# A four-layer graph network on one core: x fetched behind older adjacency codes, DMA transposes on the planner's wire, layer 3's preparation first

## The chip, the cores and the metric

The kernel runs on one NeuronCore of a Trainium2 chip. The core has a matrix engine (TensorE, PE in the profile), a vector engine (VectorE, DVE), an engine for activation functions (ScalarE, ACT), a small general one (GpSimd, POOL), and SyncE (SP), which here only issues DMAs. Each engine works through its own list of instructions in order and waits on semaphores where its operands come from another engine. Copies between the main memory and the on-chip memory are done by 16 DMA engines. The metric is the device time in microseconds; lower is better. The time before is 2350.49 us, the median of three runs (2347.99 to 2351.76).

## What is computed

32 graphs, each with 512 nodes of 256 features (`x`) and a 512x512 adjacency of zeros and ones (`adj`), go through four attention layers. Each layer normalises, clips at zero, runs its own kind of graph attention over the adjacency, and adds the result to x. All in float32. Cut to what matters:

```python
for layer in (L0, L1, L2, L3):
    h = relu(layernorm(x));  x = x + layer(h, adj)

# L0: A = softmax(h att_W h^T / 16 + mask); twice: x = tanh(A (x W + b))
# L1: Wh = h W^T; e = leaky(src_i + dst_j); softmax over neighbours; A Wh
# L2: as L1 with exp(-leaky(...)), rows divided by their sum; elu
# L3: h = feat W
#     logits = (h a_1)^T + h a_2 + (h a_12) h^T
#     e = leaky(logits); softmax over neighbours
#     elu(feat W_1 + (attention feat) W_2)
```

For layer 3 the kernel forms `M = W a_12 W^T` once, so that the logits are `feat M feat^T`. This needs W turned, a product with a_12, and a second product: the preparation that is moved below.

## The kernel before

**One plan for everything.** The kernel doesn't emit instructions as it goes. Every piece of work of every graph is an `op`: its engine ("PE", "V", "A", "G", or "D" for a DMA issued by SP), its cost as a pair (how long it holds the engine, when its result is there), what it comes after, and which buffers it uses from small pools (34 pages of 4 KB a partition, 8 PSUM banks, 5 value buffers and a few more). `Plan.order` (L134) then plays a list scheduler over all ops: each gets a due time, and on each engine the ready op with the earliest due time goes next if its buffers are free. The resulting order is the order of the instructions in each engine's list. A plan's "after" orders the issue; on the chip only true dependences of data and buffers become semaphores.

**Due times.** The ops of graph `g` get `g * apart` as their due time; the last two graphs get another distance, `apart_last`. From there each op's due time is moved forward by the costs of what follows it. `Plan.best` (L93) tries 16 values of `apart` with 4 of `apart_last`, lets `replay` (L111) play each order with the plain costs, and takes the best.

**The wire.** An op with a `size` shares one modelled wire with all others that have one: it ends when the wire has carried its bytes, at 200 bytes per ns, plus 2000 ns. Loads of x, adj and the row spreads have a size. A DMA transpose has none: it costs `D_TURN = (1310.0, 2600.0)` whatever else is on the wire.

**A graph's work.** SP fetches x (512 KB) and adj (four tiles of 256 KB). VectorE makes codes of adj (L522), DMA transposes turn them (`codeT`, L525). In each layer VectorE takes statistics of x, GpSimd the root (`rstd`), ScalarE normalises (`xn`, L573); VectorE, or ScalarE in layer 1, splits it into two 16-bit planes (L578), a DMA transpose turns each tile (`planesT`, L581), and ScalarE joins them (`hT`, L593). Then come products of features (banks f, L877), of values (banks v, L903), of scores (q, s), and attention (banks a, L761 and L838; z and o for layer 0's second convolution). Most of these are done by a scheme of seven half-size products, in which PE's next product into a bank waits until ScalarE has written the bank's content out (`fa`, `v`, `y`, `w`). Layer 3's softmax needs a maximum over rows, made with two more DMA transposes (`crest`, L1168). For graph 0, codes and layer 0's xn are turned on TensorE instead of by DMA.

**When x is fetched.** The plan lets the x of graph b go after the x of graph b-2, as soon as a page is free and fewer than seven graphs are underway.

**Preparation of the weights.** It is a part of the plan, as work of graph 0. GpSimd loads the weights after graph 0's adjacency (`load`, L345). `transposed` (L363) turns a matrix with TensorE through a bank; `product` (L379) multiplies; VectorE copies the banks out. Layer 3's W and a_12 are two such loads; W is turned (four 128x128 transposes), and two products of 256x256 give `awt` and `m3_sb`. ScalarE loads b0, its first table, and warms it up (L432 to L434) before the plan begins.

```python
    t = transposed(l3_sb, wt3, [load(l3_sb, rows_of(l3_w), "raw2")], "raw2", "raw4")
    a = product(lambda d: awt()[:, d, :], a12_sb, lambda c: wt3()[:, c, :], H,
                t + [load(a12_sb, rows_of(l3_a12), "raw3")], "raw3", "raw4", "raw5")
    a = product(lambda d: m3_sb()[:, d, :], wt3, lambda c: awt()[:, c, :], H, a, "raw4", "raw5", "raw6")
```

Of the kernel before, what the change touches and what calls it, by code (L numbers as in the profile page):

```python
# [15 lines left out]
AF = mybir.ActivationFunctionType  # L16
# [3 lines left out]
P = 128  # L20
# [27 lines left out]
A_NORM, A_JOIN, V_SPLIT = (491.0, 590.0), (620.0, 767.0), (332.0, 422.0)  # L48
D_TURN = (1310.0, 2600.0)
V_SQUARES = (180.0, 270.0)  # L50
D_OUT, D_SPREAD = (550.0, 2500.0), (550.0, 4500.0)
# [4 lines left out]
class Plan:  # L56
# [9 lines left out]

    APART, APART_LAST = [1000.0 * k for k in range(32, 64, 2)], [1000.0 * k for k in (2, 5, 8, 12)]
    HOP = 100.0
    LAND, RATE = 2000.0, 200.0
# [23 lines left out]
    def best(self, pools):  # L93
        for o in self.ops:
            o["depth"] = 0
        again = True
        while again:
            again = False
            for o in self.ops:
                depth = max((a["depth"] + 1 for a in o["after"]), default=0)  # L100
                again |= depth > o["depth"]
                o["depth"] = max(depth, o["depth"])
        apart = min(itertools.product(self.APART, self.APART_LAST), key=lambda a: self.replay(self.order(pools, *a)))
        out = self.order(pools, *apart)
        took = self.replay(out)
        assert took < float("inf"), "the plan is stuck"
        return out, took
# [25 lines left out]

    def order(self, pools, apart, apart_last):  # L134
        free = {pool: list(range(n)) for pool, n in pools.items()}
# [8 lines left out]
        for o in self.ops:  # L144
            for p in o["uses"]:
                p["users"] += 1
        last = max(o["graph"] for o in self.ops)
        for o in self.ops:
            late = max(0, o["graph"] - last + 2)
            o["due"] = (o["graph"] - late) * apart + late * apart_last  # L150
        for o in sorted(self.ops, key=lambda o: -o["depth"]):
# [57 lines left out]
def kernel(  # L209
# [153 lines left out]

    def transposed(w_sb, dst, after, *keys):
        done = []
        for c in range(HC):
            key = f"bank{next(banks)}"

            def turn(c, key):
                for r in range(HC):  # L370
                    w = w_sb()[:, r, c * P : (c + 1) * P] if len(w_sb().shape) == 3 else w_sb()[:, r, c, :]
                    nc.tensor.transpose(W[key][:, r * P : (r + 1) * P], w, ident)

            def out_of(c, key):
                p = W[key][:, : HC * P]
                nc.vector.tensor_copy(dst()[:, c], p if len(dst().shape) == 3 else p.rearrange("p (i k) -> p i k", i=2))

            a = prepare("PE", pe(nt=HC), after, partial(turn, c, key), key, *keys)
            done.append(prepare("V", V_ADD, [a], partial(out_of, c, key), key, *keys))  # L379
        return done  # L380

    def product(dst, wT, rhs, cols, after, *keys):

        done = []
        for d in range(HC):
            key = f"bank{next(banks)}"

            def multiply(d, key):
                for c in range(HC):
                    nc.tensor.matmul(W[key][:, :cols], wT()[:, c, d * P : (d + 1) * P], rhs(c),  # L390
                                     start=(c == 0), stop=(c == HC - 1))

            def out_of(d, key):
                nc.vector.tensor_copy(dst(d), W[key][:, :cols])

            cost = pe(n256=2 * HC) if cols > P else pe(nt=2 * HC)
            a = prepare("PE", cost, after, partial(multiply, d, key), key, *keys)
            done.append(prepare("V", V_ADD, [a], partial(out_of, d, key), key, *keys))
        return done
# [28 lines left out]
    for n, dst, w, key in (("w0", w0_s, w0, "raw9"), ("att", att_s, att_w, "raw10")):  # L428
# [4 lines left out]
    warm = const.tile([P, 1], F32, tag="warm", name="warm")  # L433
    nc.scalar.activation(warm, zero, AF.Exp)  # L434
    ready["w1"] = [load(w1_sb, rows_of(w1))]
# [11 lines left out]
         for i in range(2)]  # L447
# [5 lines left out]

    t = transposed(l3_sb, wt3, [load(l3_sb, rows_of(l3_w), "raw2")], "raw2", "raw4")
    a = product(lambda d: awt()[:, d, :], a12_sb, lambda c: wt3()[:, c, :], H,
                t + [load(a12_sb, rows_of(l3_a12), "raw3")], "raw3", "raw4", "raw5")
    a = product(lambda d: m3_sb()[:, d, :], wt3, lambda c: awt()[:, c, :], H, a, "raw4", "raw5", "raw6")
    ready["m3"] = seven_of(m3_sb, m3, HALF, a, "raw6")
# [18 lines left out]

    def graph(b, adj_before, x_before):

# [23 lines left out]
        def fetch_adj(t):  # L503
            nc.sync.dma_start(out=T["adj"][:, t, :], in_=adj[b, t * P : (t + 1) * P, :])


        got_x = [op("D", D_X, [x_before], partial(fetch_x, ts), "x", "ahead", size=P * H * 4 * (ts.stop - ts.start))
                 for ts in ([slice(t, t + 1) for t in range(NT)] if b == 0 else [slice(0, NT)])]
# [27 lines left out]
        for g in range(NT // 2):  # L536
            code = op("V", V_CODE, [got_adj[2 * g + 2], code], partial(classes, g), "adj", "code", "slot")
            for t in (2 * g, 2 * g + 1):
                if b:
                    coded.append(op("D", D_TURN, [code], partial(turn_code, t), "code", "codeT"))  # L540
                else:
                    key = f"bank_c{t}"
                    a = op("PE", pe(nt=NT), [code], partial(turn_code_pe, t, key), "code", key)
                    coded.append(op("V", V_MASK, [a], partial(code_of, t, key), key, "codeT"))
# [10 lines left out]
        def normed(l, xs):  # L555
# [41 lines left out]
            for g in range(NT // 2):  # L597
# [7 lines left out]
                for t in (2 * g, 2 * g + 1):  # L605
                    flat, over = f"planes{l}_{t}", f"planesT{l}_{t}"
                    a = op("A", A_NORM, [r], partial(norm, t), "x", f"xn{l}")
                    if b == l == 0:

                        key = f"bank_n{t}"  # L610
                        a = op("PE", pe(nt=2 * HC), [a], partial(turn_pe, t, key), f"xn{l}", key)
                        done.append(op("V", V_ADD, [a], partial(out_of, t, key), f"hT{l}", key))
                        continue
                    a = op("A" if l in BYACT else "V", A_JOIN if l in BYACT else V_SPLIT, [a], partial(split, t), f"xn{l}", flat)
                    a = op("D", D_TURN, [a], partial(turn, t), flat, over)
                    done.append(op("A", A_JOIN, [a], partial(join, t), over, f"hT{l}"))
# [574 lines left out]
        a = op("V", (334.0, 425.0), hi, highest, "crest3")  # L1191
        a = op("D", D_TURN, [a], partial(turn, 0, 2), "crest3")
        a = op("V", (900.0, 1000.0), [a], tops, "crest3")
        a = op("D", D_TURN, [a], partial(turn, 1, 0), "crest3")
        row = op("A", A_PRELU2, [a], leaky_row, "crest3")
# [69 lines left out]

    code, got_x = None, [None, None]
    for b in range(B):
        code, got = graph(b, code, got_x[-2])
        got_x.append(got)
# [37 lines left out]
```

## Time and profile before

| | us |
|---|---|
| median of three runs | 2350.49 |
| lowest, highest | 2347.99, 2351.76 |
| the profiled execution, its own time | 2347.43 |
| its span, first to last instruction | 2345.7 |
| VectorE busy | 2111.6 |
| ScalarE busy | 1704.1 |
| first matmul starts | 8.58 |
| last matmul ends | 2339.78 |

The span is what the trace shows; 1.7 us of the execution lie outside of it. Sums from the trace stand against 2347.43, and that execution is 3.1 us below the median. The granted clock of TensorE is 0.998 on average. Idle time of an engine that isn't the bound costs nothing by itself: GpSimd waits 1,615.7 us in all for `ve`, and nothing is late for it.

The second part of the page gives the DMA engines' share of busy time in 40 slices of 59 us. It is highest at the start, where all weights and the first graphs' inputs come in:

```profile
DMA  7431233323333233333333343233342333321221
GB/s 192 96 77 35 57 78 81 83 60 84 86 75 88 62 79 82 74 85 83 75 71 85 74 88 79 61 87 79 79 90 63 78 82 72 89 50 39 52 49 43
```

### The profile page before, as it was taken

To read this page: it belongs to the slowest core of one execution; us is meant where nothing else is said; L and a number is where in the kernel's file an instruction comes from. 1 tells how busy PE (TensorE), PEld (TensorE's weight loads), DVE (VectorE), ACT (ScalarE), POOL (GpSimd) and SP (SyncE) were. 2 spreads that over 40 slices of the span, in tenths; PEclk is the share of its full clock that TensorE was granted. 3 is DMA by queue.
4 is the path that set the end of the run, shared out by engine and by line. 5 is a ranking of instruction groups with operands and counts; after the bars stand their busy time and mean duration, and the time that the engine had idled before them with its cause. 6 is when DMAs were issued, how large, how long until landed. Compare 5 with 4: busy or idle time off the path is not lost.

```text
span 2345.7 us, 38186 instructions
## 1 busy us (share of the span) xinstructions
PE 2314.3 (99%) x13022; PEld 1999.0 (85%) x13022; DVE 2111.6 (90%) x5316; ACT 1704.1 (73%) x3273; POOL 268.6 (11%) x343
## 2 busy tenths in 40 slices
PE   7999999999999999999999999999999999999998
PEld 5888888888888898888888888988888888888887
DVE  6878899999999999999999899998999999987898
ACT  5667787667787667877777876677866778676884
POOL 3000101110110110111101111101111011010110
PEclk9999999999999999999999999999999999999999
DMA  7431233323333233333333343233342333321221
GB/s 192 96 77 35 57 78 81 83 60 84 86 75 88 62 79 82 74 85 83 75 71 85 74 88 79 61 87 79 79 90 63 78 82 72 89 50 39 52 49 43
DMA packets 429860, 178.31 MB, mean 76 GB/s; under 512 B 384128, under 2 KB 401664, under 8 KB 429664
## 3 DMA queue, kind: packets, MB, share of 16 engines
q1 hardware_dynamic: 424288, 157.51, 31.2%
q0 software_dynamic: 5232, 18.23, 2.3%
q8 instruction: 103, 1.69, 0.3%
q14 instruction: 93, 0.76, 0.1%
q10 hardware_dynamic: 144, 0.13, 0.0%
HBM read 67.64 MB, written 16.89 MB: 36 GB/s over the span
## 4 chain that ended last, share of the span: by engine, by line
PE 89%; ACT 6%; DVE 3%; DMA 2%; issue 1%; SPq 0%; ACTq 0%; DVEq 0%
PE bank_a L761 27%; PE bank_z L1012 7%; PE bank_s3p L1136 5%; PE bank_q0p L968 5%; PE bank_v0p L903 4%; PE bank_f0p L877 4%; PE bank_f3p L877 4%; PE bank_o L1030 4%; PE bank_w3p L903 4%; PE bank_a3p L838 4%; PE bank_q0q L968 3%; PE bank_s3q L1136 3%; PE bank_a3q L838 3%; PE bank_v1p L903 2%; PE bank_v3p L903 2%; PE bank_v2p L903 2%
## 5 line engine op out<-in xcount | busy, mean ns | idle before, releaser
L761 PE MATMUL bank_a<-v,e 128*128 128x258 f32 (+2 forms) x3232 | 819.3, 382 | 1.8 <-ACT e L1188 0.7
L761 PEld LDWEIGHTS bank_a<-v,e 128*128 128x128 f32 x3232 | 578.5, 191 | 78.8 <-issue 11.6
L573 ACT ACTIVATE xn<-x,off,rstd 128x256 f32<-128x256 f32 x512 | 279.4, 600 | 215.2 <-DVE off L569 214.8
L593 ACT COPY hT<-planesT 128x512 uint16<-128x512 uint16 x508 | 386.6, 773 | 48.7 <-DMA planesT<-planes 47.8
L566 POOL TENSOR_TENSOR rstd<-ve,mhalf 128x2 f32<-128x2 f32 x256 | 230.5, 912 | 1643.5 <-DVE ve L563 1615.7
L1012 PE MATMUL bank_z<-e,y 128*128 128x512 f32 x512 | 239.9, 593 | 0.9 <-ACT y L1003 0.9
L560 DVE BATCH_NORM_STATS2 st<-x 128x6 f32<-128x512 f32 x256 | 177.2, 697 | 5.8 <-DMA x<-in_x_dram 4.8
L578 DVE COPY planes<-xn 128x512 uint16<-128x512 uint16 x380 | 155.6, 421 | 25.5 <-DMA planesT<-planes 16.1
L735 ACT ACTIVATE e<-row,v 128x512 f32<-128x512 f32 x224 | 159.0, 734 | 0.2 <-DMA row<-row 0.2
L1012 PEld LDWEIGHTS bank_z<-e,y 128*128 128x128 f32 x512 | 89.7, 191 | 66.6 <-issue 57.4
L738 ACT ACTIVATE e<-e 128x1024 f32<-128x1024 f32 x128 | 137.5, 1075 | 0.1
L1030 PE MATMUL bank_o<-w_sb,zT 128*128 128x256 f32 x512 | 120.4, 379 | 0.0
L1143 DVE SCALAR_TENSOR_TENSOR e<-bank_s3p,v,mask 128x256 f32<-128x256 f32 x256 | 111.4, 477 | 8.9 <-PE bank_s3p L1136 7.8
L976 ACT ACTIVATE e<-e 128x512 f32<-128x512 f32 x124 | 78.1, 635 | 50.8 <-DVE e L987 49.6
L667 DVE TENSOR_TENSOR hs<-hT,hs 128x256 f32<-128x256 f32 x254 | 106.1, 418 | 0.5
L1030 PEld LDWEIGHTS bank_o<-w_sb,zT 128*128 128x128 f32 x512 | 95.4, 190 | 12.0
L698 ACT COPY v<-bank_v2p 128x258 f32<-128x258 f32 x128 | 47.4, 370 | 76.3 <-PE bank_v2p L903 76.0
L670 DVE TENSOR_TENSOR hs<-hT 128x512 f32<-128x512 f32 x127 | 86.9, 685 | 10.7 <-ACT hT L593 10.6
L1185 DVE TENSOR_TENSOR e<-e,crest 128x1024 f32<-128x1024 f32 x64 | 77.0, 1218 | 20.0 <-ACT crest L1179 20.0
L979 DVE TENSOR_TENSOR e<-bank_q0p,mask 128x512 f32<-128x512 f32 x124 | 84.8, 684 | 8.7 <-PE bank_q0p L968 8.5
L1231 ACT ACTIVATE r<-y,one 128x512 f32<-128x512 f32 (+1 forms) x65 | 46.5, 715 | 56.2 <-DVE y L1241 47.9
L1050 DVE SCALAR_TENSOR_TENSOR e<-codeT,e 128x1024 f32<-128x1024 bf16 x64 | 78.0, 1220 | 9.8 <-ACT e L738 9.3
(225 smaller groups left out, 5400.4 us busy)
## 6 DMA issues: line engine op xcount, KB each, us to landing
adj<-in_adj_dram SPq DMA_DIRECT2D x128, 256.0 KB
x<-in_x_dram SPq DMA_DIRECT2D x31, 512.0 KB
out_dram<-y POOLq DMA_DIRECT2D x31, 512.0 KB, 3.4
row<-row SPq DMA_DIRECT2D x56, 256.0 KB
planesT<-planes SPq DMA_TRANSPOSE x508
codeT<-code SPq DMA_TRANSPOSE x124
crest<-crest SPq DMA_TRANSPOSE x64
row<-sT SPq DMA_DIRECT2D x56, 2.0 KB
```

The costliest lines, as they stand in the source:

```text
L560: nc.vector.bn_stats(T[f"st{l}"][:, g, :], T["x"][:, two(g), :].rearrange("p t h -> p h t"))
L566: nc.gpsimd.tensor_tensor(T[f"rstd{l}"][:, two(g)], T[f"ve{l}"][:, two(g)], mhalf[:, two(g)], ALU.pow)
L573: nc.scalar.activation(T[f"xn{l}"][:, t, :], T["x"][:, t, :], AF.Relu, bias=T[f"off{l}"][:, t : t + 1], scale=T[f"rstd{l}"][:, t : t + 1])
L593: nc.scalar.copy(bits[:, :, :, t * P : (t + 1) * P], T[f"planesT{l}_{t}"].rearrange("p (b c) n -> p b c n", b=2))
L761: nc.tensor.matmul(T[key][:, : LEAD + H + 1 - lead], e(l, c)[:, t * P : (t + 1) * P], T[f"v{l}"][:, c, lead:], start=(c == 0), stop=(c == ...
L838: nc.tensor.matmul(p[:, i * WIDE : i * WIDE + k], a[:, j, i * P : (i + 1) * P], b_[:, j, :], start=fresh and i == j == 0, stop=True, skip_ ...
L877: nc.tensor.matmul(p[:, : N // 2], w[:, x - 1, :], right(x), start=fresh, stop=True, skip_group_check=True)
L903: nc.tensor.matmul(p[:, j * k : (j + 1) * k], right(x)[:, j * P : (j + 1) * P], w[:, x - 1, :], start=fresh and j == 0, stop=True, skip_gr ...
L968: nc.tensor.matmul(p[:, j * N // 2 : (j + 1) * N // 2], right(x)[:, j * P : (j + 1) * P], left(x), start=fresh and j == 0, stop=True, skip ...
L1012: nc.tensor.matmul(T[f"bank_z{k}"], T["y0"][:, c, k * P : (k + 1) * P], e(0, c), start=(c == 0), stop=(c == NT - 1))
L1030: nc.tensor.matmul(T[key][:, j * H : (j + 1) * H], T["zT"][:, k, t * P : (t + 1) * P], w1_sb[:, k, :], start=(k == 0), stop=(k == HC - 1))
L1136: nc.tensor.matmul(p[:, j * N // 2 : (j + 1) * N // 2], left(x)[:, j * P : (j + 1) * P], right(x), start=fresh and j == 0, stop=True, skip ...
```

## The change

Four things are changed. The order of all instructions is made anew by the plan, so each of them moves instructions on every engine.

1. The x of graph b now also comes after the last op of the codes of graph b-2 (`codes_before`).
2. The DMA transposes of codes, planes and crest have a `size` (128 KB each), so they share the plan's wire.
3. Layer 3's W and a_12 are loaded by ScalarE (`early`), right after b0 and before its table is loaded; the warm-up of the table comes behind them as an op of the plan. Transposing W and the two products are evacuated by ScalarE (`by="A"`) instead of VectorE.
4. `Plan.best` starts from the same grid of distances, and then moves the due times of groups of graphs: the first one to four together, and the last one to eight together, by 8, 4 and 2 us either way, keeping each move that makes `replay` shorter.

```diff
+A_ISSUE, LANDING, A_WARM = (400.0, 400.0), (0.0, 3600.0), (1480.0, 1480.0)
...
+    STEPS = [8000.0, 4000.0, 2000.0]
...
-        apart = min(itertools.product(self.APART, self.APART_LAST), key=lambda a: self.replay(self.order(pools, *a)))
-        out = self.order(pools, *apart)
-        took = self.replay(out)
+        graphs = max(o["graph"] for o in self.ops) + 1
+
+        def took_by(starts):
+            return self.replay(self.order(pools, starts))
+
+        def spread(apart, apart_last):
+            return [(g - max(0, g - graphs + 3)) * apart + max(0, g - graphs + 3) * apart_last for g in range(graphs)]
+
+        starts = min((spread(*a) for a in itertools.product(self.APART, self.APART_LAST)), key=took_by)
+        took = took_by(starts)
+        early = [slice(0, g + 1) for g in range(4)]
+        late = [slice(g, graphs) for g in range(graphs - 1, graphs - 9, -1)]
+        for step in self.STEPS:
+            for which, way in itertools.product(late[:5] + early + late[5:], (step, -step)):
+                moved = list(starts)
+                moved[which] = [t + way for t in moved[which]]
+                t = took_by(moved)
+                if t < took:
+                    starts, took = moved, t
+        out = self.order(pools, starts)
...
-            late = max(0, o["graph"] - last + 2)
-            o["due"] = (o["graph"] - late) * apart + late * apart_last
+            o["due"] = starts[o["graph"]]
...
+    def copied(by, dst, src):
+
+        if by == "A":
+            nc.scalar.copy(dst, src)
+        else:
+            nc.vector.tensor_copy(dst, src)
...
-            done.append(prepare("V", V_ADD, [a], partial(out_of, c, key), key, *keys))
+            done.append(prepare(by, A_HALF if by == "A" else V_ADD, [a], partial(out_of, c, key), key, *keys))
...
     warm = const.tile([P, 1], F32, tag="warm", name="warm")
-    nc.scalar.activation(warm, zero, AF.Exp)
+
+    def early(dst, src, key):
+
+        a = prepare("A", A_ISSUE, [], lambda: nc.scalar.dma_start(out=dst(), in_=src), key)
+        return a, prepare("L", LANDING, [a], lambda: None, key)
...
-    t = transposed(l3_sb, wt3, [load(l3_sb, rows_of(l3_w), "raw2")], "raw2", "raw4")
+    l3_here, a12_here = early(l3_sb, rows_of(l3_w), "raw2"), early(a12_sb, rows_of(l3_a12), "raw3")
+    prepare("A", A_WARM, [l3_here[0], a12_here[0]], lambda: nc.scalar.activation(warm, zero, AF.Exp))
+    t = transposed(l3_sb, wt3, [l3_here[1]], "raw2", "raw4", by="A")
     a = product(lambda d: awt()[:, d, :], a12_sb, lambda c: wt3()[:, c, :], H,
-                t + [load(a12_sb, rows_of(l3_a12), "raw3")], "raw3", "raw4", "raw5")
-    a = product(lambda d: m3_sb()[:, d, :], wt3, lambda c: awt()[:, c, :], H, a, "raw4", "raw5", "raw6")
+                t + [a12_here[1]], "raw3", "raw4", "raw5", by="A")
+    a = product(lambda d: m3_sb()[:, d, :], wt3, lambda c: awt()[:, c, :], H, a, "raw4", "raw5", "raw6", by="A")
...
-    def graph(b, adj_before, x_before):
+    def graph(b, adj_before, x_before, codes_before):
...
-        got_x = [op("D", D_X, [x_before], partial(fetch_x, ts), "x", "ahead", size=P * H * 4 * (ts.stop - ts.start))
+        got_x = [op("D", D_X, [x_before, codes_before], partial(fetch_x, ts), "x", "ahead", size=P * H * 4 * (ts.stop - ts.start))
...
-                    coded.append(op("D", D_TURN, [code], partial(turn_code, t), "code", "codeT"))
+                    coded.append(op("D", D_TURN, [code], partial(turn_code, t), "code", "codeT", size=P * N * 2))
...
-                    a = op("D", D_TURN, [a], partial(turn, t), flat, over)
+                    a = op("D", D_TURN, [a], partial(turn, t), flat, over, size=P * H * 4)
...
-        a = op("D", D_TURN, [a], partial(turn, 0, 2), "crest3")
+        a = op("D", D_TURN, [a], partial(turn, 0, 2), "crest3", size=P * N * 2)
...
-        a = op("D", D_TURN, [a], partial(turn, 1, 0), "crest3")
+        a = op("D", D_TURN, [a], partial(turn, 1, 0), "crest3", size=P * N * 2)
...
-    code, got_x = None, [None, None]
+    codes, got_x = [None, None], [None, None]
     for b in range(B):
-        code, got = graph(b, code, got_x[-2])
+        code, got = graph(b, codes[-1], got_x[-2], codes[-2])
+        codes.append(code)
```

More of the change, by code (lines that the diff above doesn't have):

```diff
@@ L132, in replay, with order @@
         return max(end.values())
-    def order(self, pools, apart, apart_last):
+    def order(self, pools, starts):
         free = {pool: list(range(n)) for pool, n in pools.items()}
@@ L146, in order @@
                 p["users"] += 1
-        last = max(o["graph"] for o in self.ops)
         for o in self.ops:
-            late = max(0, o["graph"] - last + 2)
-            o["due"] = (o["graph"] - late) * apart + late * apart_last
+            o["due"] = starts[o["graph"]]
         for o in sorted(self.ops, key=lambda o: -o["depth"]):
@@ L362, in halves, with transposed @@
         return w.rearrange("p c (i k) -> p c i k", i=2)[:, :, :, 1:]
-    def transposed(w_sb, dst, after, *keys):
+    def copied(by, dst, src):
[3 more added lines that the diff above has]
+            nc.vector.tensor_copy(dst, src)
+    def transposed(w_sb, dst, after, *keys, by="V"):
         done = []
@@ L375, in out_of, with product @@
                 p = W[key][:, : HC * P]
-                nc.vector.tensor_copy(dst()[:, c], p if len(dst().shape) == 3 else p.rearrange("p (i k) -> p i k", i=2))
+                copied(by, dst()[:, c], p if len(dst().shape) == 3 else p.rearrange("p (i k) -> p i k", i=2))
             a = prepare("PE", pe(nt=HC), after, partial(turn, c, key), key, *keys)
-            done.append(prepare("V", V_ADD, [a], partial(out_of, c, key), key, *keys))
+            done.append(prepare(by, A_HALF if by == "A" else V_ADD, [a], partial(out_of, c, key), key, *keys))
         return done
-    def product(dst, wT, rhs, cols, after, *keys):
+    def product(dst, wT, rhs, cols, after, *keys, by="V"):
         done = []
@@ L393, in out_of @@
             def out_of(d, key):
-                nc.vector.tensor_copy(dst(d), W[key][:, :cols])
+                copied(by, dst(d), W[key][:, :cols])
             cost = pe(n256=2 * HC) if cols > P else pe(nt=2 * HC)
             a = prepare("PE", cost, after, partial(multiply, d, key), key, *keys)
-            done.append(prepare("V", V_ADD, [a], partial(out_of, d, key), key, *keys))
+            done.append(prepare(by, A_HALF if by == "A" else V_ADD, [a], partial(out_of, d, key), key, *keys))
         return done
```

## The prediction

> **What bounds the kernel now.** I read the engine totals first, then the chain of waits, then TensorE's own waits, then the stages, and last the timeline where a wait stood out.
>
> ```profile
> PE 2314.3 (99%) x13022; PEld 1999.0 (85%) x13022; DVE 2111.6 (90%) x5316; ACT 1704.1 (73%) x3273; POOL 268.6 (11%) x343
> PE 89%; ACT 6%; DVE 3%; DMA 2%; issue 1%; SPq 0%; ACTq 0%; DVEq 0%
> ```
>
> TensorE is the bound: 99% busy and 89% of the chain. But "busy" hides small holes, because ends of matmuls are modelled. I want the work it must do, so I take start-to-start times from a saturated stretch of the timeline:
>
> ```profile
> 1202.07 1.03 PE L1136 MATMUL bank_s3p<-hs,fs 128*128 128x256 f32 x4
> 1202.93 1.03 PE L761 MATMUL bank_a<-v,e 128*128 128x258 f32 x4
> 1203.80 0.61 PE L903 MATMUL bank_w3p<-l_w1s,hT 128*128 128x128 f32 x4
> 1204.24 1.04 PE L761 MATMUL bank_a<-v,e 128*128 128x258 f32 x4
> ```
>
> Four passes of 256 columns take 0.86 us, four of 258 take 0.87, four of 128 take 0.44: 216, 217.5 and about 112 ns a pass; 512 columns take 429 (four in 1.72 us in the chain). Times the counts by shape (3,190 of 256, 3,232 of 257 to 259, 536 of 512, some 6,030 of 128 to 130, a few small ones) this is 2,300.2 us. Both compiled kernels hold the same passes, so neither gets below it. The span of 2,345.7 is then: 8.6 before the first matmul, 5.9 after the last, and 30.8 of holes. Summing start-to-start time minus cadence by stage, the holes are 4.4 us up to 28.5, 4.9 from there to 50, 0.6 to 100, 11.0 from 100 to 2150 and 10.0 after that. Everything this change can win is in those 45 us; its own first-order effect on TensorE's work is nil. The stages and the waits agree:
>
> ```profile
> 0.00:8.58 8.58, 0.00 (x1) 0.01 (x1) 2.28 (x8) 2.14 (x4) 2.38 (x17) 1.00 0.70 218
> 8.58:28.50 19.92, 19.38 (x64) 10.95 (x65) 15.58 (x50) 8.97 (x16) 12.03 (x16) 1.00 0.87 235
> 28.50:50.00 21.50, 18.80 (x74) 13.88 (x75) 15.01 (x47) 15.11 (x31) 6.71 (x9) 0.92 0.79 172
> ```
> ```profile
> PE bank_n L586 <- ACT xn L573: 9.0, 2, 8.6
> PE bank_f3p L877 <- ACT fa L887: 5.2, 7, 1.2
> PE bank_f0p L877 <- ACT fa L885: 2.0, 1, 2.0
> PE bank_a3p L838 <- DVE e L814: 1.3, 1, 1.3
> ```
>
> Columns of a stage: its time, then busy time of PE, PEld, DVE, ACT, POOL, then clock, DMA share, GB/s. The DMA engines are 70 to 87% busy in the first 50 us. The start's chain names what they hold up, and the timeline shows what is behind the second wait, for one graph in the middle:
>
> ```profile
> 20.17 7.08 DMA planesT<-planes
> 27.28 0.77 ACT hT L593
> 28.08 6.04 DMA planesT<-planes
> ```
> ```profile
> 1327.40 0.77 ACT L593 COPY hT<-planesT 128x512 uint16<-128x512 uint16 x1 [1.22 <-DMA planesT<-planes]
> 1329.18 0.48 ACT L887 ACTIVATE fa<-bank_f3p,l_u 128x256 f32<-128x256 f32 x1
> 1329.71 0.70 PE L877 MATMUL bank_f3p<-hT,m 128*128 128x256 f32 x2 [0.88 <-ACT fa L887]
> ```
>
> Two DMA transposes took 7.1 and 6.0 us at the start. Later ScalarE, which works in order, stood 1.22 us before a late transpose, evacuated the f3 bank late, and TensorE stood 0.88 us. That stall comes back every fourth graph (at 758, 1044, 1330 and 1616 us: 0.57, 0.90, 1.04, 1.35, together 3.9).
>
> **What the Trainium skill says.** "DMA: Bandwidth & Descriptors", section "Queues, rings and completion order": each DMA engine serves the rings of SP and ScalarE in turn, by packets. So loads on ScalarE's ring take bandwidth from x on SP's; the trace of before has only 0.13 MB on ScalarE's ring and can't show it. Its section "Issuing engines are not separate DMA queues" says that a second issuer saves only issue time. "TensorE: Matmul & The Clock Gate", section "What's actually happening": the array starts at half clock until about 3.4 us of busy time. The trace agrees: graph 0's first eight 256-column passes take 3.65 us (456 ns each against 216).
>
> **The change part by part.**
>
> *Layer 3's W and A first.* Removed from GpSimd: two issues at 26.4 and 27.2 us (0.74 and 0.77 us); GpSimd is 11% busy, so that is nothing. Added on ScalarE: two issues at the 0.41 us of its b0 issue, so table load (1.28) and warm (0.20) end near 3.5 us instead of 2.7; ScalarE is idle until 7.92 anyway: nothing. Moved: 4 transposes and 16 passes, 4 x 0.112 + 16 x 0.216 = 3.9 us of TensorE, from a full stretch to the front, where it has 8.6 us of idleness; and six 128x256 copies, 0.42 each on VectorE, to ScalarE at about 0.38, 2.3 us. In the compiled order ScalarE makes four of these copies before graph 0's first xn, so graph 0 waits for W, the transposes, A and the first product. The cost: W issued near 1.2 to 1.6 lands near 5.5 to 6.5 us (x's first tiles, issued from 0.74, were used at 5.46, and 512 KB more now share the engines: at 235 to 380 GB/s 1.4 to 2.2 us for whatever comes behind, x of graph 1 among it). Transposes and copies to about 7.8, eight passes at the cold 0.456 to 11.4, so xn starts near 11.5 where it was 7.92, and the first n at 12.2 where it was 8.58. That is 3.6 lost. Against it: 3.9 of work is done, the cold stretch is paid by it and not by graph 0 (8 x 0.24 = 1.9), and the 0.4 waits between the n pairs are filled by the second product (some 0.5). Net gain 2.7; I take 3. Ends: W at 4.5 us gives 5; A late by 3 us gives 0; VectorE waiting for x of graph 1 before the second offset, behind all loads, gives -2.
>
> *x behind the codes two graphs back.* This is in the plan alone. In the compiled SP queue it moves x of graphs 2 and 3 from before graph 0's adjacency to behind graph 1's first transposes and behind adj 1, and x 4 to 6 behind adj 3 to 5. From graph 8 on each x stands at the same place as before (x 19 still between layer 1's and layer 2's transposes), so there it is nothing. At the start four x of 0.5 MB leave the first 24 us, some 7 us of the engines at 300 GB/s. The transposes of 7.1 and 6.0 us should fall towards the 3.3 to 4.4 us that the same wait has later in the chain. The holes from 28.5 to 50 are 4.9; ScalarE's wait for those transposes ended 2.2 of it, the reduced clock after it about 1.5. I take 2.5 of it as won. Against: graphs 2 to 5 filled TensorE while graph 0 went through its chain alone, and they now come later. I placed both orders on the cadence scale: graph 3's first f0 moves from 43 to 84 us, graph 4's from 134 back to 112; graph 0 has v1 at 63 (was 59), but f3 at 165 (was 176). Distances in graph 0's chain (o0 to v1: 21 us against 19; a1 to v2 17 against 20; v2 to a2 9 against 15) leave the 4 to 5 us of leaky, exp and mask covered. So -0.5. Sum of this part 2; ends -4 (fillers missing) and 4.
>
> *Transposes on the plan's wire, and due times moved graph by graph.* No instruction is added; the order changes all the way. In the table of stages the order of before repeats every four graphs, the new one every graph (f3 of graphs 12, 13, 14, 15 at 1013, 1084, 1156, 1227 us). At the f3 of graph 16, ScalarE now writes two fa blocks before it turns to hT of graph 20 (before: one, then hT, exp, the second), and SP issues both of graph 20's first transposes ahead of the row spread, not one. That is the stall above, so I count 3.9 as mostly gone, and half of the other 7.1 between 100 and 2150: 3.5 + 3.5 less 2 for new ones = 5. Ends: 9 and, by the rival below, -14. In the tail the last 22 us of matmuls are the same in both orders, one by one, and stages from graph 29's a2 on stand within 1 us; the 5.9 after the last matmul stay. Of the 10 us of holes I take 1; ends -3 and 4.
>
> Sum: 3 + 2 + 5 + 1 = 11 on the profiled execution's 2347.4 (span 2345.7 and 1.7 around it): 2336.4. The median of the runs shown is 3.1 above that execution, so 2339.5 by the median; I say 2339. What is late next is TensorE itself, still with some 20 us of holes.
>
> **Rivals.** (A) Only the start gains, the rest stays as it is: 5 us, 2345.5. For it: the tail hardly moves, the middle was planned already. Against: the order that stalled is rearranged at exactly that place. (B) Slower: one stall in every graph. Graph 12's stages in the new order stand within 1 us of those of before's graph 12, and that is one of the stalling ones; the others are now copies of it. If f3 or another bank then waits 0.9 us in each of some 20 graphs, that is 18 us in place of 3.9, against 6 won elsewhere: 2350.5 + 14 - 6 = 2358.5. It decides from 20 x s - 3.9 - 6 > 4.7, so s above 0.73 us a graph. For it: VectorE is 46 to 48 us busy in 50 there, little slack. Against: the two changes of queue order named above, and before's 50 us windows with no hole at all. (C) Prep in front costs graph 0 more than it frees (W or A at 8 us or later): start -4, middle +5, rest 1: 2348.5. (D) It doesn't do what it says: the x rule is inert after the start; that is in the forecast already.
>
> **How the numbers follow.** Forecast, 2334 to 2344: 0.56. A: 0.17. B: 0.15. C: 0.12. Low end: all good ends together (5 + 4 + 9 + 4 = 22) would give 2328.5; I take 2330. High end: 2353 leaves B's upper part out. A measurement of this kernel can tell 0.2%, 4.7 us, from no change: 2345.8 and 2355.2 are the borders. Faster: forecast 0.56, most of A 0.11, a little of C 0.04: 0.71. Same: rest of A, most of C, B's lower edge: 0.15. Slower: 0.14.
>
> **What would show it.** Right: first matmul near 6 us, sixteen passes with about 450 ns at the front, first xn at 11 to 12, attention of graph 0 (a0) near 27 to 28 though 3.9 us more work precede it; planesT pairs of 3 to 4 us there; f3's 5.2 us of waits under 2.5; DMA share of the second slice lower. Wrong: a PE wait repeated every 71.4 us; PE idle between 40 and 130 us; W's landing after 8 us.

## The result and the profile after

| | before | after |
|---|---|---|
| median of the runs (four each) | 2351.12 | 2325.88 |
| lowest, highest | 2347.99, 2355.23 | 2325.32, 2327.81 |
| ratio of the times, 95% interval | | 0.9892 [0.9878, 0.9907] |
| the profiled execution, its own time | 2347.43 | 2327.81 |
| TensorE's holes, by the sum used in the prediction | 30.8 | 12.7 |

The kernel became 25 us faster; 11 were forecast, and 2325.88 lies below the range of 2330 to 2353. In the profiled executions the difference is 19.6 us. The other 5.6 come from where these two executions stand among their runs: before's is 3.7 below the median of its four runs here (3.1 below that of the three known then), after's is the slowest of its four, 1.9 above theirs.

The first, second and fourth parts of the page of after (engine totals, slices, shares of the chain):

```profile
PE 2307.2 (99%) x13022; PEld 1996.3 (86%) x13022; DVE 2113.0 (91%) x5310; ACT 1720.1 (74%) x3279; POOL 257.5 (11%) x341
...
DMA  6441233423333323333233333233332333321221
...
PE 92%; ACT 3%; DVE 2%; DMA 1%; issue 0%; SPq 0%; ACTq 0%; DVEq 0%
```

The same 13,022 passes run. The chain has 3% more of TensorE, 3% less of ScalarE. The second DMA digit stays at 4. The stages of the start (columns as before: its time, busy time of PE, PEld, DVE, ACT, POOL, clock, DMA share, GB/s):

```profile
0.00:8.58 8.58, 1.31 (x5) 0.94 (x6) 0.76 (x2) 2.08 (x4) 1.00 (x15) 1.00 0.68 214
8.58:28.50 19.92, 19.89 (x75) 12.40 (x76) 16.67 (x52) 10.42 (x21) 10.38 (x13) 1.00 0.81 208
28.50:50.00 21.50, 21.50 (x95) 15.88 (x94) 13.08 (x45) 11.11 (x22) 3.88 (x5) 1.00 0.46 108
```

From 28.5 to 50 TensorE is full (18.8 of 21.5 before), and the DMA engines are 46% busy there instead of 79%. TensorE's waits of after (what it waited for: total, times, longest):

```profile
PE bank_w L396 <- DMA raw_w<-in_L_gnn_W_dram: 7.2, 1, 7.2
PE bank_f3p L907 <- ACT fa L917: 0.9, 2, 0.7
```

The stall at f3 has gone from 5.2 us in seven waits to 0.9 in two. Where it came from, the longest pieces of the two chains tell. Before had these, one every four graphs, and the next at 1608.91 (start, length, what):

```profile
752.19 3.34 DMA planesT<-planes
...
1037.05 4.35 DMA planesT<-planes
...
1322.89 4.49 DMA planesT<-planes
```

Among the 40 longest pieces of after's chain no `planesT` is left; its only DMAs are layer 3's W at the start and a few others:

```profile
1.17 5.93 DMA raw_w<-in_L_gnn_W_dram
...
1021.95 4.74 DMA codeT<-code
```

One line misleads. This is ScalarE's wait for the transposes in before, and then in after:

```profile
ACT hT L593 <- DMA planesT<-planes: 47.8, 58, 3.4
```
```profile
ACT hT L623 <- DMA planesT<-planes: 47.0, 52, 6.5
```

The sum is the same. I therefore took every join (ScalarE's `hT`) that had waited for its transpose, and measured from the start of SP's issue to the start of the join. Before, 36 of 61 took over 3 us (median 3.41, longest 7.78); after, 11 of 53 (median 2.49, longest 5.08). The quick ones are joined after 2.42 to 2.55 us. In before, 24 of the 36 late ones had a DMA other than a transpose issued in the 4 us ahead of them, and 2 of the 18 quick ones; in after, 2 of the 11 late ones, so loads aren't the whole of it. ScalarE still waits for 47 us. That it now does so mostly where TensorE needs nothing from it is inferred from TensorE's own waits; it wasn't followed wait by wait.

By stage, with the prediction's sum of holes (start-to-start time less cadence; a few hundredths below zero are rounding of the cadence), one profiled execution each:

| us | before first matmul | to 28.5 | to 50 | to 100 | 100-2150 | after 2150 | after last matmul |
|---|---|---|---|---|---|---|---|
| before | 8.6 | 4.4 | 4.9 | 0.6 | 11.0 | 10.0 | 5.9 |
| after | 7.2 | 3.2 | 0.0 | 0.6 | 3.5 | 5.3 | 5.8 |
| won | 1.3 | 1.2 | 4.9 | -0.1 | 7.5 | 4.7 | 0.1 |

The prediction's sum counts slow passes as holes too. Twice in before, right after stalls, the granted clock (third column from the right) was about one half for 3.4 us:

```profile
36.20:39.60 3.40, 3.40 (x12) 2.85 (x11) 2.24 (x11) 3.13 (x8) 3.28 (x5) 0.50 0.58 79
2200.20:2203.70 3.50, 3.50 (x13) 3.06 (x13) 3.50 (x6) 2.41 (x5) 0.35 (x1) 0.51 0.17 33
```

Most passes of 257 and 258 columns start every 427 to 431 ns there instead of every 217, which makes about 1.7 us of the 4.9 and 1.7 of the 10.0. The execution of after has no such stretch before its last matmul.

### The profile page after: what moved, and what is told of

It is laid out like the page before. It is cut to its first block, busy times and chain, and to the rows that moved or that the text cites. A ratio compares the mean times of both kernels' runs of the same rounds, so it can differ in the third digit from the quotient of the medians.

```text
span 2326.0 us, 38151 instructions
## 1 busy us (share of the span) xinstructions
PE 2307.2 (99%) x13022; PEld 1996.3 (86%) x13022; DVE 2113.0 (91%) x5310; ACT 1720.1 (74%) x3279; POOL 257.5 (11%) x341
## 4 chain that ended last, share of the span: by engine, by line
PE 92%; ACT 3%; DVE 2%; DMA 1%; issue 0%; SPq 0%; ACTq 0%; DVEq 0%
PE bank_a L791 28%; PE bank_z L1042 8%; PE bank_s3p L1166 5%; PE bank_q0p L998 5%; PE bank_o L1060 4%; PE bank_v0p L933 4%; PE bank_f0p L907 4%; PE bank_w3p L933 4%; PE bank_f3p L907 4%; PE bank_a3p L868 4%; PE bank_s3q L1166 3%; PE bank_q0q L998 3%; PE bank_a3q L868 3%; PE bank_v1p L933 2%; PE bank_v2p L933 2%; PE bank_v3p L933 2%
## 5 line engine op out<-in xcount | busy, mean ns | idle before, releaser
L596 POOL TENSOR_TENSOR rstd<-ve,mhalf 128x2 f32<-128x2 f32 x256 | 222.4, 899 | 1737.6 <-DVE ve L593 1537.6
L623 ACT COPY hT<-planesT 128x512 uint16<-128x512 uint16 x508 | 375.9, 771 | 47.4 <-DMA planesT<-planes 47.0
L608 DVE COPY planes<-xn 128x512 uint16<-128x512 uint16 x380 | 155.4, 419 | 13.6 <-DMA planesT<-planes 8.2
L700 DVE TENSOR_TENSOR hs<-hT 128x512 f32<-128x512 f32 x127 | 86.9, 684 | 11.7 <-ACT hT L623 11.3
L1080 DVE SCALAR_TENSOR_TENSOR e<-codeT,e 128x1024 f32<-128x1024 bf16 x64 | 78.0, 1219 | 12.5 <-ACT e L768 12.4
L1111 DVE SCALAR_TENSOR_TENSOR e<-codeT,e 128x1024 f32<-128x1024 bf16 x64 | 77.9, 1218 | 6.6 <-ACT e L768 6.5
```

The lines of the kernel that those rows point to most:

```text
L596: nc.gpsimd.tensor_tensor(T[f"rstd{l}"][:, two(g)], T[f"ve{l}"][:, two(g)], mhalf[:, two(g)], ALU.pow)
L623: nc.scalar.copy(bits[:, :, :, t * P : (t + 1) * P], T[f"planesT{l}_{t}"].rearrange("p (b c) n -> p b c n", b=2))
```

## The experiments

The theory after the result: the transposes' `size` brings most of it, at the start and in the tail too, since it tells the planner which transposes will be late (in the tail this is a guess: before has one late join there). The rival: each part has its own share at its own place, as the prediction had it.

**One part left out of the change.** The edits to the changed kernel, one for each run (`no_early` also puts back the two GpSimd loads, VectorE's copies and the early warm-up):

```diff
# no_gate
-        got_x = [op("D", D_X, [x_before, codes_before], partial(fetch_x, ts), "x", "ahead", size=...)
+        got_x = [op("D", D_X, [x_before], partial(fetch_x, ts), "x", "ahead", size=...)
# no_early
-    t = transposed(l3_sb, wt3, [l3_here[1]], "raw2", "raw4", by="A")
+    t = transposed(l3_sb, wt3, [load(l3_sb, rows_of(l3_w), "raw2")], "raw2", "raw4")
# no_size, at all four DMA transposes
-                    a = op("D", D_TURN, [a], partial(turn, t), flat, over, size=P * H * 4)
+                    a = op("D", D_TURN, [a], partial(turn, t), flat, over)
# no_search
-    STEPS = [8000.0, 4000.0, 2000.0]
+    STEPS = []
```

> All of the change but the rule that x comes behind the codes two graphs back. Theory P (each part has its own place): the early x are back in front of the first adjacency, transposes of 6 to 7 us come back there and the holes from 0 to 50 us go from 3.2 to about 8; the middle and the tail stay; 2331. Theory O (the gain is the order that the search of due times finds, the parts hardly matter): within 2 us of 2326.

> All of the change but layer 3's early loads and preparation. Theory P: first matmul back at 8.6 us, graph 0's first passes at 450 ns, 3.9 us of preparation back in the full stretch; the start loses 3 to 5 us and nothing else moves; 2330. Theory O: within 2 us of 2326.

> All of the change but the size of the DMA transposes in the plan. Theory P: the middle's stalls on late planesT come back, holes from 100 to 2150 us go from 3.5 to about 9 or 10; start and tail stay; 2332. Theory O: the search finds as good an order; within 2 us of 2326.

> All of the change but the moves of single due times; the grid alone. Theory P: only the two ends can change, the tail's holes go from 5.3 back to 9 or 10, the middle stays at 3.5; 2331. Theory O: most of the gain is lost, the four-graph pattern of stalls is back; 2340 or more.

**One part alone, on the kernel before.** The same four edits the other way; `only_early`, `only_size` and `only_gate` have `STEPS = []`.

> Before with nothing new but the moves of single due times. Leaving this part out of the change cost 4 us. Theory P (parts add up): 4 to 5 us are won, 2344, and the holes from 28.5 to 50 us stay near 4.9. Theory R (parts stand in for one another: any one of them breaks before's bad order): 10 us or more, 2338 or less.

> Before with nothing new but layer 3's early loads and preparation. Theory P: 2 us, 2347 or so: first matmul at 7.3 us, the rest as before, tail's holes 10. Theory R: a new order altogether, 2340 or less, tail's holes under 7.

> Before with nothing new but the size of the DMA transposes. Theory P: 5 us, 2344, all of it in the middle (100 to 2150 us: holes from 11 to 6), tail's holes 10. Theory R: 2338 or less, tail's holes under 7 too.

> Before with nothing new but x behind the codes two graphs back. Theory P: nothing, 2349, as leaving it out cost nothing. Theory R, and my prediction's own account of the start: the holes from 28.5 to 50 us fall from 4.9 to under 2, 2345 or less.

Medians, ratios to before in the same series (its median 2348.37 there, 2349.82 here), and the holes of the profiled execution:

| | median | ratio [95%] | 28.5-50 | 100-2150 | after 2150 |
|---|---|---|---|---|---|
| no_gate | 2325.75 | 0.9902 [0.9887, 0.9917] | 0.6 | 0.6 | 5.3 |
| no_early | 2327.85 | 0.9911 [0.9897, 0.9926] | 0.0 | 0.5 | 5.3 |
| no_search | 2330.24 | 0.9923 [0.9907, 0.9940] | -0.1 | 5.8 | 5.6 |
| no_size | 2331.01 | 0.9924 [0.9910, 0.9939] | -0.1 | 5.0 | 6.2 |
| only_size | 2331.71 | 0.9920 [0.9905, 0.9935] | -0.1 | 2.6 | 4.9 |
| only_search | 2343.26 | 0.9969 [0.9957, 0.9982] | 5.5 | 11.3 | 6.2 |
| only_gate | 2344.01 | 0.9972 [0.9961, 0.9983] | 1.9 | 10.7 | 8.6 |
| only_early | 2346.08 | 0.9984 [0.9977, 0.9991] | 9.6 | 12.0 | 10.3 |

The holes are those of one execution each, which lies 4.0 us above the median in `only_early`, 2.4 above in `only_search`, and within 1 us of it in the others. The changed kernel wasn't run again in these series; `no_gate`, whose 2325.75 is next to its 2325.88, stands in for it.

Neither theory held throughout. `only_size` and `only_gate` came out as R had them, `only_search` and `only_early` nearer to P; and without the search the tail's holes stayed at 5.6, where P had 9 to 10.

Three things follow. The size alone wins 18 us of 25. Without it, the three others together still win 17.4 of them, about the sum of what they win singly (6.6 + 5.8 + 3.7 = 16.1). And all four together win less than 18 + 16: the parts stand in for one another. The table shows where. The holes from 28.5 to 50 are removed by the size alone, and in `no_size` without it (where the x rule alone takes 3 of the 4.9); the tail's are halved by the size alone, and 3.8 of them go by the search alone. So leaving the x rule out costs nothing, layer 3's preparation 2 us, the search and the size 4 to 5 each.

`no_size` shows more: its joins are as late as before's (30 of the 51 that waited took over 3 us, median 3.54; between 100 and 2150 us, 25 of 41, before's 28 of 50), and ScalarE waits longer for them, but TensorE's wait at f3 for `fa` is 1.8 us, before's 5.2:

```profile
ACT hT L623 <- DMA planesT<-planes: 50.7, 47, 6.4
PE bank_f3p L907 <- ACT fa L917: 1.8, 2, 1.0
```

So the time can fall by 17 us while the late joins stay. Less of what TensorE needs stands behind them, as f3's row suggests. The size is one way to such an order, and not the only one.

How can the size clear the start, when x still stands early? SP's queue in before, then in `only_size` (start, length, what, count):

```profile
18.57 0.57 SPq L501 DMA_DIRECT2D x<-in_x_dram  x1
20.17 1.20 SPq L581 DMA_TRANSPOSE planesT<-planes  x1
21.54 0.45 SPq L504 DMA_DIRECT2D adj<-in_adj_dram  x1
22.10 1.20 SPq L581 DMA_TRANSPOSE planesT<-planes  x1
23.35 0.81 SPq L501 DMA_DIRECT2D x<-in_x_dram  x1
```
```profile
19.07 0.57 SPq L530 DMA_DIRECT2D x<-in_x_dram  x1
21.77 0.34 SPq L533 DMA_DIRECT2D adj<-in_adj_dram  x1
22.16 0.44 SPq L530 DMA_DIRECT2D x<-in_x_dram  x1
27.05 2.50 SPq L610 DMA_TRANSPOSE planesT<-planes  x2
```

Before, two transposes are laced between the loads; with the size, they go as a pair behind them. ScalarE's list follows. First before, with the two late joins each ahead of a block of e that graph 0's attention needs, then `only_size`:

```profile
27.28 0.77 ACT L593 COPY hT<-planesT 128x512 uint16<-128x512 uint16 x1 [3.37 <-DMA planesT<-planes]
27.92 0.59 ACT L941 ACTIVATE e<-bank_q 128x512 f32<-128x512 f32 x1
29.88 0.77 ACT L593 COPY hT<-planesT 128x512 uint16<-128x512 uint16 x1 [1.37 <-DMA planesT<-planes]
30.52 0.58 ACT L941 ACTIVATE e<-bank_q 128x512 f32<-128x512 f32 x1
```
```profile
27.51 0.60 ACT L970 ACTIVATE e<-bank_q 128x512 f32<-128x512 f32 x1
27.99 1.09 ACT L602 ACTIVATE xn<-x,off,rstd 128x256 f32<-128x256 f32 x2
29.20 0.60 ACT L970 ACTIVATE e<-bank_q 128x512 f32<-128x512 f32 x1
...
35.44 0.76 ACT L622 COPY hT<-planesT 128x512 uint16<-128x512 uint16 x1
...
37.05 0.75 ACT L622 COPY hT<-planesT 128x512 uint16<-128x512 uint16 x1
```

In `only_size` all four blocks of e are out by 29.8 us, and the joins come later and wait for nothing. `only_early` is the counterpart, in an execution 4.0 us above its median: layer 3's loads stand in front, the transposes keep their fixed cost, and ScalarE stands for 7 and 3 us before e (and TensorE, through VectorE's e, for 5.1 us in all):

```profile
31.75 0.77 ACT L623 COPY hT<-planesT 128x512 uint16<-128x512 uint16 x1 [6.95 <-DMA planesT<-planes]
32.39 0.58 ACT L971 ACTIVATE e<-bank_q 128x512 f32<-128x512 f32 x1
36.01 0.76 ACT L623 COPY hT<-planesT 128x512 uint16<-128x512 uint16 x1 [3.04 <-DMA planesT<-planes]
```

**Which side of the size counts.** A size does two things to a transpose in the plan: it waits for the bytes ahead of it, and it keeps the wire from what comes behind. These four are built as `only_size` is. 1310.0 marks a DMA transpose. Shown are the lines in `Plan.order`; `replay` has the same.

```diff
# wait_only: it waits, and does not hold the wire
-                        wire = max(wire, now) + o["size"] / self.RATE
-                        until = wire - now + self.LAND + o["late"]
+                        there = max(wire, now) + o["size"] / self.RATE
+                        until = there - now + self.LAND + o["late"]
+                        if o["plain"][0] != 1310.0:
+                            wire = there
# hold_only: it holds the wire, its own end stays fixed
-                        until = wire - now + self.LAND + o["late"]
+                        if o["plain"][0] != 1310.0:
+                            until = wire - now + self.LAND + o["late"]
# margin: no size, every transpose 1 us later
-D_TURN = (1310.0, 2600.0)
+D_TURN = (1310.0, 3600.0)
# planes_size: the size on the 508 planes transposes alone, codes and crest without
```

> Only the size of the DMA transposes, and of it only one side: a transpose waits in the plan for the bytes ahead of it, but keeps nothing else waiting. Theory W (what counts is that the plan knows a transpose to be late behind a load, so ScalarE's in-order list asks for it later): as with the whole size, 2332, joins that wait do so for transposes of about 2.5 us. Theory H (what counts is that loads are seen to be late behind transposes): 2345 or more.

> The other side: a transpose takes its share of the plan's wire, so loads come later in the plan, but its own end stays at the fixed 2600 ns. Theory W: 2345 or more, with transposes of 3.5 us and more among the waits. Theory H: 2332.

> Before, with the fixed end of every DMA transpose in the plan at 3600 ns and not 2600; no size, nothing else new. Theory W in its strict form (the plan must know which transposes are late): 2340 or more, since all are put off alike. Theory M (any margin does it): 2334 or less.

> The size for the 508 transposes of planes alone, not for codes and crest (188). Theory W: most of the gain, 2335 or less, because ScalarE's joins are what waits in order. If the row maxima's transposes or the codes matter as much: 2340 or more.

| | median | ratio to before (2349.14) [95%] | joins over 3 us, of those that waited |
|---|---|---|---|
| planes_size | 2330.12 | 0.9918 [0.9904, 0.9933] | 16 of 49 |
| wait_only | 2340.95 | 0.9964 [0.9951, 0.9977] | 19 of 47 |
| margin | 2343.39 | 0.9976 [0.9967, 0.9985] | 18 of 21 |
| hold_only | 2350.12 | 1.0007 [0.9998, 1.0015] | 30 of 57 |

The planes transposes are all of it: 19 us, where the size on all kinds gave 18. Waiting alone gives 8 us, which fits neither expectation (and its joins are those of an execution 4.0 us below its median); holding alone gives nothing, the two together (`only_size`) 18. So in these orders neither side does it alone. A flat microsecond on each gives 6; it makes waiting joins rarer (21 instead of 61) but 18 of the 21 are long ones. Being careful with all of them alike is therefore not enough. That telling the late from the quiet ones is what the size adds fits these runs, but isn't shown: `no_size` has more late joins than `margin` and is 12 us faster.

**Further, from the changed kernel.** The first two keep the whole order, with one extra copy from DRAM to DRAM behind each x from graph 6 on, of 512 KB and of 16 KB; it is no part of the reference. The third lowers the wire's speed in the plan, the fourth searches on.

```diff
# more_traffic; small_traffic copies 16 rows
+                nc.sync.dma_start(out=away.rearrange("(t p) h -> p t h", p=P), in_=x[b].rearrange("(t p) h -> p t h", p=P))
# rate_150
-    LAND, RATE = 2000.0, 200.0
+    LAND, RATE = 2000.0, 150.0
# finer
-    STEPS = [8000.0, 4000.0, 2000.0]
+    STEPS = [8000.0, 4000.0, 2000.0, 1000.0, 500.0]
-        late = [slice(g, graphs) for g in range(graphs - 1, graphs - 9, -1)]
+        late = [slice(g, graphs) for g in range(graphs - 1, 3, -1)]
```

> The changed kernel, its order held, and behind each x from graph 6 on one more DMA of 512 KB from the same x to an unused place in main memory; the plan doesn't know of it. Theory W: the transposes of layer 2 just behind it land 2 us late or more, ScalarE stands for them, and TensorE's holes grow: 8 us or more against the kernel with the small DMA. If the order has enough room for late transposes: under 3 us.

> The same extra DMA at the same place, but of 16 KB: what the additional issue on SP costs. Either way within 2 us of 2326.

> The changed kernel with the plan's wire at 150 bytes per ns and not 200, so that transposes look later still behind loads. If what is left in the middle is late transposes: 2323 to 2325. If not: within 2 us of 2326 or above.

> The changed kernel with more moves of due times: steps of 1 and 0.5 us too, and every graph from 4 on. If the search is what limits it: 2321 to 2324. If the plan's picture of the chip is: within 2 us of 2326.

Medians: 2326.47 (0.9901 [0.9886, 0.9916]), 2326.31 (0.9901 [0.9886, 0.9916]), 2332.72 (0.9927 [0.9910, 0.9943]) and 2326.55 (0.9902 [0.9887, 0.9917]). The additional 13.6 MB cost nothing, which tested less than it was meant to: behind x the next planes transpose is issued some 9 us later, so the copies fall into a quiet place. A wire at 150 in the plan costs 7 us; its holes from 100 to 700 are 7.2 us, after's 1.3. The finer search found nothing more.

**Loads doubled where transposes follow.** The next two kernels have the extra copy (256 KB, again no part of the reference) behind each adj tile from graph 6 on, in the kernel before and in the changed one. TensorE's, ScalarE's and VectorE's lists are unchanged in both; SP has 104 more issues.

```diff
+            if 6 <= b:
+                away = dram.tile([P, N], I32, tag=f"away{t}", name=f"away{t}_{b}")
+                nc.sync.dma_start(out=away, in_=adj[b, t * P : (t + 1) * P, :])
```

> The kernel before, its order held, with the same extra DMAs. Theory W: this order asks for transposes at the first moment, so it loses more than the changed one does under the same load, 10 us or more, 2360 or above. If late transposes don't cost TensorE time: within 3 us of 2350.

> The changed kernel, its order held, and behind each adjacency tile from graph 6 on one more DMA of the same 256 KB to an unused place in main memory, of which the plan knows nothing (104 in all). Theory W: transposes behind them land late, holes of TensorE come up in the middle; more than 5 us, 2331 or above. If the new order has room for late transposes: within 3 us of 2326.

TensorE's waits for ScalarE's `fa` at f3, the row that the prediction followed; before with the copies, then the changed kernel with them:

```profile
PE bank_f3p L880 <- ACT fa L890: 13.8, 14, 3.5
```
```profile
PE bank_f3p L910 <- ACT fa L920: 2.0, 3, 0.7
```

Before went to 2362.71 (1.0052 [1.0036, 1.0069]), 12.4 us more than its 2350.27 in this series. The changed kernel went to 2337.42 (0.9946 [0.9932, 0.9961]), 11.5 more than its 2325.88. Joins over 3 us rose from 36 to 59 and from 11 to 42. Before pays most at the row where it stalled already, 5.2 us becoming 13.8; but that execution took 2367.82, 5.1 above its median, so a usual run pays less. In the changed kernel the row grew by only 1.1 us of the 8.8 between the two profiled executions; the rest is many small holes from 100 to 2150. So with the order held, more loads make joins later and TensorE slower; that the late transposes bring all of it isn't shown, since the copies can delay other transfers too. And at the medians the changed order isn't the more robust one: other loads than it was planned for spoil it as they spoil the other. The 104 issues (some 0.55 us each) are in both and weren't tried apart, beyond the 26 of `small_traffic` that cost nothing.

No kernel here beats the changed one by more than its runs spread.

## Why the prediction was wrong

**The direction and the mechanism were right.** An `hT` join behind a late transpose in ScalarE's ordered list holds up `fa`, and that holds up f3: this was named as what bounds the middle, f3's 5.2 us were to fall under 2.5 and fell to 0.9, TensorE's work stayed 2,300.2 us, and rival B (a stall in every graph) didn't come: the holes from 700 to 1700 are 0.0. One sign of being right failed, the lower DMA share of the second slice: the digit stayed at 4, with 114 GB/s where before had 96.

**Layer 3's W and A first: +3 forecast, 2.5 found** (1.3 before the first matmul, 1.2 up to 28.5), and 2.0 by `no_early`. Each point in time came about a microsecond later than stated, from W's landing at 7.1 instead of 5.5 to 6.5 (start, length, engine, line, what, in after):

```profile
7.24 1.08 PE L396 MATMUL bank_w<-ident,raw_w 128*128 128x128 f32 x4 [7.24 <-DMA raw_w<-in_L_gnn_W_dram]
7.57 0.70 DVE L590 BATCH_NORM_STATS2 st<-x 128x6 f32<-128x512 f32 x1 [6.69 <-DMA x<-in_x_dram]
...
12.44 1.09 ACT L603 ACTIVATE xn<-x,off,rstd 128x256 f32<-128x256 f32 x2
...
13.17 0.85 PE L616 MATMUL bank_n<-ident,xn 128*128 128x128 f32 x4
...
29.06 1.03 PE L791 MATMUL bank_a<-v,e 128*128 128x257 f32 x4
```

x's first tiles, too, were used at 7.57 instead of 5.46. The Trainium skill's "DMA: Bandwidth & Descriptors", "Queues, rings and completion order", has each engine serve the two rings in turn; the 2.1 us here agree with it. Graph 0's first attention starts at 29.1 (27 to 28 forecast), with 3.9 us more work ahead of it. The prediction's 456 ns for a cold pass is too much: it divides 3.65 us by eight, which holds a late start of the second pass and the modelled end of the last; from start to start they are 427 ns, and nine of the sixteen passes ran that slowly, not all.

**x behind the codes: 2 forecast, 0 within this change.** The 4.9 us of holes from 28.5 to 50 went, all of them where I took 2.5, and the fillers' -0.5 didn't show. But `no_gate` has 0.6 there and the same time: with the size in the plan the rule isn't needed. Alone it wins 5.8, so less traffic at the start is a cause that works; it isn't the only one that does.

**The step that failed is the sum for "Transposes on the plan's wire, and due times moved": "3.5 + 3.5 less 2 for new ones = 5" and "of the 10 us of holes I take 1".** The middle gave 7.5, and the tail 4.7, above the end of 4 that I had left it; with the 2.9 more from 28.5 to 50, where `only_size` shows the same part at work, these are 9.1 us that were mis-sized, all one way. Three judgements made them small. In the middle I counted the one stall that repeats, halved everything else and took 2 off for new stalls, though the other holes were in the same lists. I sized the tail from its last 22 us, which are the same in both orders, while its holes stood elsewhere: by the start-to-start sums, 5.6 us of the 10 lie from 2180 to 2220 and 3.1 from 2260 to 2280, and after has 1.1 and 2.1 at the matching places 20 us earlier. Some 1.7 of the 5.6 are the passes at half clock, which I had counted at the start alone. And I looked at the start only for what fewer bytes would do, not for what else ScalarE could do while a transpose was late.

**A second term was the 3.1 us** by which before's profiled execution lay below the median. I added it to the forecast as a property of the kernel. It was chance: the changed kernel's own profiled execution lay 1.9 above its median, and those of the experiments lie from 4.0 below to 5.1 above theirs. The two are 5 us of the 13 by which the forecast missed.

Left open: how the size, or the search, shortens the tail (no DMA stands behind the longest remaining holes; they are banks waiting for ScalarE's or VectorE's copies); how much of this term is the size and how much the search, since no run leaves out both and keeps the rest; and why the two sides of the size need each other, since the order couldn't be held while the size was changed, so part of each median is the luck of one order.

## What to carry to other kernels

When a planner orders in-order engines, give every transfer that shares the memory traffic the same model, and check the predicted against the traced latency for each kind: here one kind with a fixed 2.6 us, which took 2.4 at best and up to 7.8 among the start's loads, was worth 18 us when nothing else was changed. Judge a wait by what stands behind it in its engine's list, not by its total: 47.8 and 47.0 us of the same wait went with 2347 and 2328. When a change reorders a whole program, add up the holes by stage and ask for each of them whether its cause can survive, before halving what hasn't been looked at; and don't carry one execution's offset from its median to another kernel.

## What the runs showed of the hardware

A DMA transpose of a 128x512 tile of 16-bit values within the on-chip memory holds SP for 1.19 us in the median. The quickest are joined 2.42 to 2.55 us after their issue began; the late ones mostly after 3 to 5, at the start after 7.8 in before and 11.4 in `only_early`.

Runs of one kernel differ by unequal amounts: before's 28 runs in one series go from 2346.8 to 2354.8, `only_early`'s 20 from 2343.4 to 2350.6, while the changed kernel's four stay within 2.5 us. Late joins alone don't make the difference: `no_size` has 30 of them, and its four runs stay within 1.5. But in `only_early` the ten runs with a mean granted clock of 0.999 took 2343.4 to 2346.1, and the four with 0.997 took 2347.9 to 2350.6. Whether the lower clock makes the longer run, or more stalls make both, isn't shown.

The granted clock can fall to one half without a long stall. Ahead of before's second such stretch TensorE was busy for 17.8 of 20.2 us, and the two longest holes there were 1.3 and 0.8 us.

TensorE's first 256-column passes of after start every 427 ns, and the first at 216 starts 5.5 us after the first matmul, with some 0.4 us of idleness between. The Trainium skill's "TensorE: Matmul & The Clock Gate", "What's actually happening", gives about 3.4 us. Here it took longer, in before too (7.1 us, with some 0.8 of idleness), and the measurement decides: the prediction's "The trace agrees" holds for the half rate, not for the 3.4 us.
